# Routed tiles transposed in halves of 64 rows, in a kernel of two small transformer layers

## The chip, the cores and the metric

The kernel runs on one core of one Trainium2 chip. A core has TensorE (matmuls, "PE" in the profile, with its weight loads as "PEld"), VectorE ("DVE"), ScalarE ("ACT"), GpSimd ("POOL"), and SyncE ("SP"), whose queue issues most DMAs here. The metric is the device time of one execution in microseconds (us), lower is better. Before the change it is 555.82 us, the median of 8 runs that lie between 554.58 and 558.35.

## The reference, cut to what matters

The input is x of 8 x 256 tokens with 128 features, all in float32. Two layers follow each other; each normalises x and adds an attention part and a feed-forward part to it.

```python
xn = _layernorm(x)
x = x + scan_layer(xn) + ternary_ffn(xn)        # layer 0
xn = _layernorm(x)
x = x + ttt_attention(xn) + moe(xn)             # layer 1

# moe, the part around the change: E = 8 experts, 2 of them for each token, FF = 512
scores = sigmoid(xf @ gate_w.T + gate_b)
top_scores, top_idx = top_k(scores, 2)
hdn = gelu(xf @ w1[e] + b1[e])                  # for each expert e
y = hdn @ w2[e] + b2[e]
out = sum of the two chosen y, weighted, + 0.1 * shared expert
```

The attention of layer 1 keeps a small weight matrix W for each of 16 heads and updates it by a gradient step for each chunk of 64 tokens, so chunk n + 1 needs the W that chunk n has left.

## The kernel before, in words

**Tiles.** A tile is 128 rows of tokens on the 128 partitions. Layer 1's attention runs as 16 "units" (4 chunks x 4 pairs of batch rows), one after the other in a software pipeline: in each turn of the loop at L1303 one unit does its keys and states, the one before it its gradient and its update of W, and the one before that its outputs. The matrices between these steps go through TensorE, VectorE and GpSimd in turn.

**The routed experts.** Each token is written twice to a buffer in DRAM (xg_dram), sorted by expert. NJ = 39 tiles of 128 rows are then read back, three at a time: GJ = 3, NG = 13 groups. For a group, routed_tokens (L824) loads xg, three tiles with a token in each partition. routed_tokens_T (L832) transposes them, since the first matmul needs the features on the partitions: TensorE's transposes at L837 write one bank of PSUM, pxg, and one copy of ScalarE at L853 brings it to xgT in SBUF. For each tile j, routed_first (L855) multiplies xgT with the expert's first matrix (phd, four matmuls at L861) and applies the gelu (rhid, four ScalarE instructions at L866), and routed_second (L871) multiplies with the second one (pyr, L876). routed_sums (L882) adds the bias on VectorE (ys, L887), and a scattering DMA of GpSimd (L163) writes the rows to y_dram. routed_step (L909) strings these together: the transposes of group g + 1 are asked for in the step of tile 3g + 1, ahead of phd of tile 3g + 2 and of pyr of tile 3g + 1. The expert's weights, ew, come by DMA (L821) three tiles ahead, into four buffers.

**The order.** The order on VectorE and SP is that of the code. On TensorE and ScalarE a scheduler that knows the dependencies places the instructions, until the last unit, from where these two go by hand as well. The routed steps are the filler of the units' turns: `filler()` (L1319) puts a given number of them between the units' steps (the tables SLOTS and ROUTED).

**PSUM.** Eight banks: a pool "two" of two pairs of banks for the units, and a pool "bank" of four single banks for all else: pxg, phd, pyr, the units' po (L1258), and the shared expert's tiles. A tile of the pool takes over the bank of an earlier one, and TensorE waits until that one has been read.

**What stands elsewhere in the code.** transpose_pairs (L985) transposes the units' keys and outputs (pxkT, poT) in halves of 64 rows, the two halves into two banks; TensorE's line is L995, ScalarE's copies L999. Further lines that the prediction names: L982 (pk, pv: the units' projections, 512 columns wide), L1011 (pq), L1026 (pz, pzq: W applied, 64*64 matmuls), L1193 and L1200 (pw, pb), L1212 and L1213 (W and B on VectorE), L1094 (u), L1247 (o), L1259 and L1266 (po), L1181, L1273 (the residual). L496 is a copy of the first layer norm.

Of the kernel before, what the change touches and what calls it, by code (L numbers as in the profile page):

```python
# [17 lines left out]
P = 128  # L18
B, S, D = 8, 256, 128
# [16 lines left out]
GJ = 3  # L36
# [42 lines left out]
def tile_two_layers(ctx: ExitStack, tc: tile.TileContext, t: dict, out: bass.AP):  # L79
    nc = tc.nc  # L80
# [10 lines left out]
    def bank(name):  # L91
        return ps1.tile([P, 512], F32, tag="bank", name=name)
# [4 lines left out]
    def resident(name, shape):  # L97
        return const.tile(shape, F32, tag=name, name=name)
# [14 lines left out]
    ident = resident("ident", [P, P])  # L113
# [308 lines left out]
    with (  # L422
# [149 lines left out]
        for two in range(NBP // 2):  # L572

            pxp = bank("pxp").rearrange("p (b s) -> p b s", b=2)
            for half in range(2):
                for i in range(2):
                    b = 2 * (2 * two + i)
# [69 lines left out]
        for par in range(2):  # L647
            q = slice(par * 64, par * 64 + 64)
# [166 lines left out]
    ew, xg, xgT, hidden, ysum, unsummed, ats = {}, {}, {}, {}, {}, [], {}  # L815
# [15 lines left out]

    def routed_tokens_T(g):  # L832
        if g < NG:
            pt = bank("pxg")[:, : GJ * P].rearrange("p (j q) -> p j q", j=GJ)
            src = xg.pop(g)
            for j in range(GJ):
                nc.tensor.transpose(pt[:, j, :], src[:, j, 0:D], ident)  # L837
            ats[g] = side["moe"].tile([P, GJ], I32, tag="ats", name="ats", bufs=3)

            def places():  # L840

                first = small.tile([P, GJ], F32, tag="first", name="first")
                nc.vector.tensor_tensor(
                    first, src[:, :, D + 1], tile_rank[:, g * GJ : (g + 1) * GJ], ALU.is_equal
                )
                nc.vector.scalar_tensor_tensor(
                    ats[g], first, -float(B * S), src[:, :, D], ALU.mult, ALU.add
                )
                known.append(g)

            quiet.append(places)
            xgT[g] = side["moe"].tile([P, GJ, P], F32, tag="xgT", name="xgT")
            nc.scalar.copy(xgT[g], pt)  # L853

    def routed_first(j):  # L855
        w = ew[j]
# [52 lines left out]
    def routed_step(j):  # L909
        if j == 0:  # L910
            routed_tokens_T(0)
            routed_first(0)
        if j % GJ == 0:
            routed_tokens(j // GJ + 2)
        routed_sums()
        expert_weights(j + 3)
        if j % GJ == 1:
            routed_tokens_T(j // GJ + 1)
        if j + 1 < NJ:
            routed_first(j + 1)  # L920
        if j < NJ:
            routed_second(j)
# [380 lines left out]
    for u in range(units - 1):  # L1303
# [3 lines left out]
        z, g, o = live.get(u), live.get(u - 1), live.pop(u - 2, None)  # L1307
# [82 lines left out]
    o, g, z = live[units - 3], live[units - 2], live[units - 1]  # L1390
# [202 lines left out]
```

## Time and profile before

| what | us |
|---|---|
| median of 8 runs | 555.82 (554.58 to 558.35) |
| the profiled execution | 557.71 |
| its span, first to last instruction | 556.0 |
| TensorE busy | 524.4 (94%) |
| VectorE busy | 405.6 (73%) |
| GpSimd busy | 293.4 (53%) |
| ScalarE busy | 259.1 (47%) |
| TensorE busy from 290 to 480 us, where the transposes lie | 184.3 of 190 |
| the 39 transposes, first and last start | 296.4 and 472.9 |

A line of instructions in the profile names the line of the code, the engine, the operation, the tile that is written <- those read, the shape, and the count. A busy TensorE is a row of pipelined matmuls: one takes 0.27 us from start to end, but the next starts after 0.11 us, so start times are compared here and not durations. A matmul of float32 shows as two records, a transpose as one. In the timeline a row begins with its start in us and the time from its first start to its last end; a bracket at its end gives the idle time before it and what ended it.

### The profile page before, as it was taken

The page shows a single profiled execution, that of the slowest core. Times are in us where ns is not written, and L with a number is a line of the kernel's source. Part 1 is how long each engine was busy: PE and PEld are TensorE (multiplying, and loading weights), DVE is VectorE, ACT ScalarE, POOL GpSimd, SP SyncE. Part 2 cuts the span into 40 slices and gives each one's busy share as a digit, 9 for nine tenths or more (in the row PEclk, how much of TensorE's full clock was granted, in tenths as well). Part 3 has the DMA queues.
Part 4 walks back from the last instruction along what each step waited for, and adds up shares of the span by engine and source line. Part 5 has one row for each costly group of instructions (what it writes and reads, how often), then busy time and mean ns, then how long its engine had stood idle before and what let it go on. Part 6 is the DMA issues. An engine that isn't in the chain of part 4 may idle for free. (4 is left out here: it accounts for less than half of the span.)

```text
span 556.0 us, 14196 instructions
## 1 busy us (share of the span) xinstructions
PE 524.4 (94%) x5891; PEld 363.9 (65%) x5891; DVE 405.6 (73%) x649; ACT 259.1 (47%) x472; POOL 293.4 (53%) x258
## 2 busy tenths in 40 slices
PE   6999999999999999999988999999999999998785
PEld 3443655465455645667767888887887777878674
DVE  5599353556951377585889798979889877769995
ACT  4655544324430452232625364462645454462695
POOL 6208102862491125725486576575865747384852
PEclk9999999999999999999999999999999999999899
DMA  7910200000000000000053554452543534300402
GB/s 271 399 62 27 63 1 2 30 10 2 11 16 16 1 0 25 17 0 2 16 176 103 146 153 135 150 182 94 171 153 106 155 115 139 101 17 5 133 22 77
DMA packets 25201, 45.89 MB, mean 83 GB/s; under 512 B 3876, under 2 KB 16298, under 8 KB 24625
## 3 DMA queue, kind: packets, MB, share of 16 engines
q1 hardware_dynamic: 22864, 40.75, 22.7%
q0 software_dynamic: 2272, 4.24, 2.3%
q8 instruction: 46, 0.75, 0.6%
q14 instruction: 19, 0.15, 0.1%
HBM read 38.30 MB, written 7.13 MB: 82 GB/s over the span
## 5 line engine op out<-in xcount | busy, mean ns | idle before, releaser
L293 PE MATMUL pm<-g,h 128*128 128x512 f32 x256 | 113.6, 595 | 0.0
L175 POOL TENSOR_TENSOR rstd<-rs_v,neg_half 128x16 f32<-128x16 f32 x31 | 93.1, 3003 | 2.6
L293 PEld LDWEIGHTS pm<-g,h 128*128 128x128 f32 x256 | 48.2, 190 | 59.7 <-issue 57.0
L1118 POOL TENSOR_TENSOR gx<-xh,gam 128x1024 f32<-128x1024 f32 (+1 forms) x17 | 37.9, 2228 | 68.7 <-DVE er L1117 51.1
L866 ACT ACTIVATE rhid<-phd,ew 128x128 f32<-128x128 f32 x156 | 44.6, 373 | 40.1 <-PE phd L861 27.3
L297 ACT ACTIVATE g<-pm,cols 128x512 f32<-128x512 f32 x32 | 22.0, 687 | 75.9 <-PE pm L293 75.9
L174 POOL TENSOR_SCALAR rs_v<-var 128x16 f32<-128x16 f32 x31 | 7.3, 235 | 82.8 <-DVE var L1054 82.1
L1054 DVE TENSOR_REDUCE var<-sq 128x16 f32<-128x1024 f32 (+1 forms) x33 | 38.9, 1181 | 9.4 <-ACT sq L1048 9.4
L163 POOL DMA_INDIRECT y_dram<-ys,ats x39 | 40.7, 1044 | 8.9 <-issue 8.8
L861 PE MATMUL phd<-xgT,ew 128*128 128x128 f32 x312 | 43.1, 280 | 1.2 <-DMA ew<-in_moe_w 1.1
L861 PEld LDWEIGHTS phd<-xgT,ew 128*128 128x128 f32 x312 | 39.1, 192 | 7.4 <-issue 4.9
L1048 ACT ACTIVATE sq<-o 128x1024 f32<-128x1024 f32 (+1 forms) x17 | 17.1, 1011 | 53.6 <-DVE o L1037 53.6
L876 PE MATMUL pyr<-ew,rhid 128*128 128x128 f32 x312 | 41.4, 276 | 0.0
L163 POOL DMA_INDIRECT xg_dram<-xn,slot x32 | 35.9, 1121 | 8.6 <-issue 7.4
L1119 POOL TENSOR_TENSOR gx<-gx,u 128x1024 f32<-128x1024 f32 (+1 forms) x17 | 38.4, 2257 | 1.3
L876 PEld LDWEIGHTS pyr<-ew,rhid 128*128 128x128 f32 x312 | 38.0, 192 | 0.6 <-issue 0.5
L1094 DVE TENSOR_TENSOR u<-rows_b,pv 128x1024 f32<-128x1024 f32 x16 | 19.5, 1219 | 19.6 <-PE pv L982 19.6
L1266 PE MATMUL po<-wo,oT 128*128 128x128 f32 x256 | 31.4, 276 | 0.7 <-ACT oT L999 0.7
L982 PE MATMUL pk<-wk,xnT 128*128 128x512 f32 x64 | 31.4, 610 | 0.7 <-DVE xh L1037 0.5
L982 PE MATMUL pv<-wv,xnT 128*128 128x512 f32 x64 | 31.4, 614 | 0.0
L1011 PE MATMUL pq<-xnT,wq 128*128 128x256 f32 x128 | 30.8, 383 | 0.6 <-DVE B L1213 0.6
L1266 PEld LDWEIGHTS po<-wo,oT 128*128 128x128 f32 x256 | 29.9, 192 | 1.1 <-ACT oT L999 1.1
(233 smaller groups left out, 1058.7 us busy)
## 6 DMA issues: line engine op xcount, KB each, us to landing
ew<-in_moe_w SPq DMA_DIRECT2D x39, 578.0 KB, 3.9
xg<-xg_dram SPq DMA_DIRECT2D x39, 65.0 KB, 2.5
h<-in_h SPq DMA_DIRECT2D x2, 1024.0 KB, 8.5
yc<-y_dram SPq DMA_DIRECT2D x6, 256.0 KB, 4.1
rows_g<-in_rows_g SPq DMA_DIRECT2D x1, 1024.0 KB, 7.7
rows_b<-in_rows_b SPq DMA_DIRECT2D x1, 1024.0 KB, 7.8
w<-in_w SPq DMA_DIRECT2D x3, 256.0 KB, 3.0
x<-in_x SPq DMA_DIRECT2D x3, 256.0 KB, 5.6
```

What stands on the lines that cost most here:

```text
L163: ins = nc.gpsimd.indirect_dma_start(**what).ins
L175: turn[:] = [nc.gpsimd.tensor_tensor(dst, v[:, :width], neg_half[:, :width], ALU.pow).ins]
L293: nc.tensor.matmul(pm, lhsT=w[:, k, m * P : (m + 1) * P], rhs=s[src][:, k, :], start=(k == 0), stop=(k == 3),)
L861: nc.tensor.matmul(ph[:, ms], lhsT=w[:, ms], rhs=xgT[j // GJ][:, j % GJ, :], start=True, stop=True)
L866: nc.scalar.activation(hid[:, m, :], ph[:, ms], AF.Gelu, bias=w[:, C_EB1 + m : C_EB1 + m + 1])
L876: nc.tensor.matmul(py, lhsT=hid[:, m, :], rhs=w[:, C_EW2 + m * D : C_EW2 + (m + 1) * D], start=(m == 0), stop=(m == 3),)
L982: nc.tensor.matmul(pp[:, j, :], lhsT=xT, rhs=w[:, j * 512 : (j + 1) * 512], start=True, stop=True)
L1011: nc.tensor.matmul(pq[:, i, :], lhsT=wq[:, (h0 + i) * P : (h0 + i + 1) * P], rhs=xnT[n][:, 2 * half : 2 * half + 2, :], start=True, stop=True,
L1054: nc.vector.tensor_reduce(v[:, heads], sq[:, heads], AX.X, ALU.add)
L1118: nc.gpsimd.tensor_tensor(g, xh, gam2[:, k], ALU.mult)
L1119: turn[:] = [nc.gpsimd.tensor_tensor(g, g, self.t[:, k], ALU.add).ins]
L1266: nc.tensor.matmul(self.po, lhsT=self.oT[:, hp, :], rhs=wo[:, hp, :], start=False, stop=(hp == HH - 1),)
```

## The change

Each tile is transposed in two halves, rows 0 to 63 and 64 to 127. The first halves of a group's three tiles go to one bank, the second halves to another one, so a group takes two banks of the pool of four in place of one. Six transposes of 64 rows take the place of three of 128, and two copies of ScalarE (128 partitions x 3 x 64 elements each) that of one of 128 x 384; each writes its half of xgT's columns.

```diff
     def routed_tokens_T(g):
         if g < NG:
-            pt = bank("pxg")[:, : GJ * P].rearrange("p (j q) -> p j q", j=GJ)
             src = xg.pop(g)
+
+            pts = []
+            for b in range(2):
+                pts.append(bank("pxg")[:, : GJ * 64].rearrange("p (j q) -> p j q", j=GJ))
             for j in range(GJ):
-                nc.tensor.transpose(pt[:, j, :], src[:, j, 0:D], ident)
+                for b in range(2):
+                    rb = slice(b * 64, b * 64 + 64)
+                    nc.tensor.transpose(pts[b][:, j, :], src[rb, j, 0:D], ident[rb, rb])
...
             xgT[g] = side["moe"].tile([P, GJ, P], F32, tag="xgT", name="xgT")
-            nc.scalar.copy(xgT[g], pt)
+            for b in range(2):
+                nc.scalar.copy(xgT[g][:, :, b * 64 : b * 64 + 64], pts[b])
```

In the built program VectorE, SP and GpSimd keep their order. On TensorE the scheduler makes these moves besides: in group 1 one matmul of pq goes ahead of phd; in group 4 the first half-transpose of pxkT goes ahead of pyr; in group 11 the six halves stand with the three first ones in front, and of the phd matmuls that stand between other work there one is placed later, as is one of the next tile.

## The prediction

> **What bounds the kernel now.** I read the page's busy shares first, then the table of windows for the stretch in which the change lives, then the tile view of pxg, and last the timeline around single groups. "Group g" (0 to 12) is one call of routed_tokens_T: three routed tiles.
>
> The chain of waits on the page is no help: it holds 1 us. The busy shares and the windows (sum of each engine in us per stretch) are:
>
> ```profile
> PE 524.4 (94%) x5891; PEld 363.9 (65%) x5891; DVE 405.6 (73%) x649; ACT 259.1 (47%) x472; POOL 293.4 (53%) x258
> ...
> 290.00:360.00 70.00, 67.39 (x981) 54.70 (x982) 62.71 (x83) 35.26 (x79) 43.70 (x28) 1.00 0.47 143
> 360.00:420.00 60.00, 59.04 (x910) 47.50 (x902) 50.54 (x70) 28.70 (x64) 42.50 (x29) 1.00 0.46 145
> 420.00:480.00 60.00, 57.88 (x881) 47.22 (x879) 47.63 (x64) 30.82 (x69) 37.28 (x26) 1.00 0.41 130
> ```
>
> From 290 to 480 us TensorE is busy 184.3 of 190 us at full clock, VectorE 160.9, ScalarE 94.8. All 13 groups lie there. So what lengthens TensorE's queue lengthens the kernel, unless a wait of TensorE on something else follows soon and swallows it. What the diff touches is small:
>
> ```profile
> L837 PE MATMUL pxg<-ident,xg x39: 272/273/331, 296.4 to 472.9; 128*128 128x128 f32 x39
> L853 ACT COPY xgT<-pxg x13: 463/478/498, 299.0 to 473.8; 128x384 f32<-128x384 f32 x13
> ```
>
> 273 ns is a latency; transposes start 0.11 us apart (303.31 to 303.63 for three). The whole step holds TensorE for 13 x 0.33 = 4.3 us.
>
> **The transposes themselves.** The kernel already has the new form, 64 rows into two banks, in L995 (poT, pxkT). TensorE's timeline around group 4:
>
> ```profile
> 346.62 0.49 PE L837 MATMUL pxg<-ident,xg 128*128 128x128 f32 x3
> 346.95 1.06 PE L861 MATMUL phd<-xgT,ew 128*128 128x128 f32 x8
> 347.84 1.06 PE L876 MATMUL pyr<-ew,rhid 128*128 128x128 f32 x8
> 348.83 0.71 PE L995 MATMUL pxkT<-ident,xk 64*128 64x64 f32 x16
> 349.48 0.70 PE L982 MATMUL pv<-wv,xnT 128*128 128x512 f32 x1
> ```
>
> Differences of the start times give all prices. phd to pyr, eight records of full matmuls, is 0.89; pyr to pxkT, also eight, is 0.99: entering the 64-row form costs 0.10. Sixteen halves take 0.65 until the next engine operation starts (348.83 to 349.48). They go in pairs: at 307.24 the first pair starts, at 307.35 the second, and further ones 0.06 apart. Three pairs are then 0.65 - 5 x 0.062 = 0.33 or 0.34, as much as the three full transposes. After a 64-row block the first full matmul is long: phd at 307.89, behind poT, needs 0.99 for its eight records (pyr starts at 308.88), against 0.89. Leaving therefore costs another 0.10. So a group between full matmuls pays 0.33 before and 0.10 + 0.33 + 0.10 = 0.53 after: +0.20 us. It has two neighbours of another kind:
> - behind poT (groups 3 and 8) the kernel is in the form already: before, 330.93 to 331.95 for 16 halves and three transposes, 1.02; after, 0.65 + 3 x 0.062 = 0.83, and phd later by 0.10: -0.09.
> - behind the 64*64 matmuls of L1026 (groups 2, 7, 10) the three transposes take 0.39 (440.53 to 440.92), already with a slow first. After: 0.33 + 0.10, with the same way in: +0.05. That a change from 64*64 to 64*128 costs what one to 128*128 costs is assumed; L1181 to L995 at 540.74 has the same 0.15 us start to start.
>
> The trace speaks here against a rule. The Trainium skill, TensorEngine Tiling (Array Packing), section Overview, gives operands of at most 64 up to twice the speed; alone it would make the sum 13 x 0.165 = 2.1 us less, an estimate from that page. The same page, Tiling Modes, says that a change of the tiling mode drains TensorE, which is what the 0.10 at the entry looks like, and its first gotcha that row tiling raises the pressure on PSUM.
>
> **The banks.** "bank" is a pool of four. A group now takes two, so each later tile in the ring waits for another predecessor. I compared the waits of the two built programs, and put each new one against the start and end times of before. The second half's bank waits for ys (L887) or a gelu (L866) that ended 1.8 to 4.3 us earlier in groups 2 to 9; phd's and pyr's waits on ys, a gelu or the residual (L1273) ended 0.6 to 2.8 us earlier. These cost nothing: the cover is that slack. pyr's new wait for the group's first copy is different, since ScalarE is in order. Group 3:
>
> ```profile
> 331.94 1.02 ACT L999 COPY oT<-poT 128x1024 f32<-128x1024 f32 x1
> 332.84 0.50 ACT L853 COPY xgT<-pxg 128x384 f32<-128x384 f32 x1
> ...
> 332.85 1.06 PE L876 MATMUL pyr<-ew,rhid 128*128 128x128 f32 x8
> ```
>
> The copy stands behind two long ones (xqT, oT) and starts at 332.84; pyr is ready at 332.85. A copy of 128x192 has no row. Copies of 256 (L496, 372 ns) and 384 (482 ns) give 0.86 ns an element, so 0.32 us; not below 0.28 (the cheapest small ScalarE row, 283 ns for 128x96), not above 0.37 (256). Its end, 333.16, and 0.05 for the semaphore (gelu ends at 452.33, phd starts at 452.38) put pyr at 333.21: +0.36. A matmul that waited is followed late (452.38: four records up to poT take 0.65, 0.10 more than full ones with the entry), +0.10. Group 8 is the same (copy 405.44, pyr 405.45). So +0.46 each, -0.09 included; bounds +0.3 (no late second, shortest copy) and +0.55. Behind pyr queue the mix of L1259/L1266 and pw, for which VectorE waits (W at 337.07), so nothing hides it.
>
> Group 4: its copy starts at 347.73 and would be done at 348.05; pyr comes at 347.84 + 0.20. But the scheduler also puts the first half of pxkT ahead of pyr: one more way in and out, 0.10 + 0.15 + 0.10 = +0.35, below which the wait disappears. Bounds 0.1 (it merely replaces the wait) and 0.4. In group 1 one pq matmul moves ahead of phd and covers the gelu it now waits for (303.89). In group 11 the second halves wait for the gelu that ended at 452.33, and phd for the first copy: about +0.35 at 452.4.
>
> **The copies.** ScalarE's copies start 0.37 us before the next operation (332.84 to 333.21). Two of 192 take about 0.05 more than that: 13 x 0.05 = 0.7 us on an engine half idle. The later gelus serve a pyr that runs a step later. Without that cover (group 3's gelus on the path) it would be 0.1 a group. SP's, POOL's and VectorE's orders are unchanged; no DMA is added or moved.
>
> **What swallows some of it.** TensorE's waits behind groups:
>
> ```profile
> 379.56 0.72 PE L995 MATMUL poT<-ident,o 64*128 64x64 f32 x16 [0.56 <-DVE o L1247]
> ...
> 426.50 0.72 PE L995 MATMUL poT<-ident,o 64*128 64x64 f32 x16 [0.42 <-ACT rhid L866]
> ...
> 458.41 0.91 PE L861 MATMUL phd<-xgT,ew 128*128 128x128 f32 x6 [1.12 <-DMA ew<-in_moe_w]
> ```
>
> Before 379.56 VectorE ran without a gap from 369.1; so group 6 (372.4) is hidden. The same for group 9 (423.8), where o ended at 426.35. The weights of 458.41 were issued at 452.93, behind a ys that stands behind u, which waited for pv (450.25), not for group 11: its 0.35 is hidden. Group 0 is followed by a wait of 1.3 for xh. If those covers go, +0.2, +0.2, +0.35 and +0.2 come back. All other delays lie ahead of a VectorE wait on TensorE (u on pv at 351.50, 400.12, 450.25, 477.53), so both shift and nothing catches up.
>
> **The sum.** Groups 1, 4, 5, 12: 4 x 0.20 = 0.80; 2, 7, 10: 0.15; 3 and 8: 0.92; group 4's extra excursion 0.35; copies 0; groups 0, 6, 9, 11: 0. Together +2.2 us. The profiled execution took 557.71 (span 556.0 and 1.7 around it) and would take 559.9. It stands 1.9 above the median of the runs, 555.82; the same +2.2 on the median is 558.0, +0.4%. 0.3%, about what a measurement of this kernel can tell from no change, is 1.7 us.
>
> **The rivals.**
> - It comes to nothing. The late second matmul may belong to longer blocks, a short block may enter cheaper, and more of TensorE's 5.5 us of waits in this stretch may swallow. With the entry alone (4 x 0.10), the waits 2 x 0.3 and 0.1 for group 4: +1.1, less 0.4 swallowed: 556.5. For it: each term is a tenth. Against: entry and exit show at every L995 block of this stretch.
> - Faster. If three pairs are left and entered without a stop, they cost 0.19 in place of 0.33: 13 x 0.14 = -1.8, and 554.0 if pyr also finds its copy done. It decides where a way in and out together is below 0.14; the rows say 0.20, and 3 and 8 would still wait.
> - The ring of four is too short. If VectorE falls over 2 us behind in its ys additions, the second half's bank waits stop TensorE in seven or eight groups, at about 0.5 us each: +4 more, 562. It needs ys later by the slack of 1.8 to 4.3 us; delays of TensorE move VectorE along, which speaks against.
>
> **How the numbers follow.** My forecast has 0.60 (own range 557.2 to 559.5), nothing 0.20, faster 0.10, the ring 0.10. The range of 554.8 to 560.8 leaves out most of the ring case and part of the faster one. Slower by over 0.3% (above 557.5): most of the forecast and the ring, 0.66; within: the second case and the low end of the forecast, 0.23; faster 0.11.
>
> **What would show it.** L853 has 26 copies near 0.32; pxg has 78 halves, three pairs 0.06 to 0.11 apart; phd behind them takes 0.99; pyr of groups 3 and 8 idles about 0.4 with ScalarE's xgT as releaser; the waits at 379.56, 426.50 and 458.41 shrink. TensorE's stretch from 290 to 480 is 2 us longer, the tail behind it the same. I am wrong if TensorE waits for ys at the halves, or if that stretch keeps its length.

## The result, and the profile after

| | kernel before | changed kernel |
|---|---|---|
| median of the runs, us | 555.69 (46 runs, 554.05 to 558.35) | 558.16 (16 runs, 557.08 to 560.65) |
| profiled execution, us | 557.71 | 558.34 |
| its span, us | 556.0 | 556.6 |

The ratio is 1.0042, with a 95% interval of 1.0032 to 1.0052: slower by 2.5 us of median. The prediction said 558.0. Note at once what does not fit: the two profiled executions lie only 0.6 us apart, where the prediction added 2.2 to the one and expected 559.9 of the other. That gap is taken up below.

First the busy shares of the page and the table of windows of the changed kernel (length, then busy us and instructions of PE, PEld, DVE, ACT, POOL, then the granted TensorE clock, the DMA share, GB/s):

```profile
PE 526.0 (95%) x5930; PEld 362.7 (65%) x5930; DVE 405.2 (73%) x649; ACT 260.2 (47%) x485; POOL 293.8 (53%) x258
...
290.00:360.00 70.00, 67.08 (x961) 53.44 (x960) 61.49 (x81) 35.65 (x84) 43.76 (x28) 1.00 0.47 142
360.00:420.00 60.00, 58.92 (x937) 47.30 (x937) 49.90 (x71) 27.98 (x66) 40.78 (x28) 1.00 0.46 146
420.00:480.00 60.00, 59.19 (x890) 47.10 (x889) 48.60 (x63) 31.44 (x71) 39.07 (x27) 1.00 0.41 129
```

TensorE works 39 instructions more, ScalarE 13 more; VectorE, POOL and the moved bytes stay. From 290 to 480 us TensorE is busy 185.2 us instead of 184.3, in a stretch of the same length that holds slightly less of the program. The clock is full here in both.

The tile view of pxg shows the new form (minimum, median and maximum in ns, first and last start), and who waited for it:

```profile
L842 PE MATMUL pxg<-ident,xg x78: 221/223/273, 296.5 to 473.9; 64*128 64x64 f32 x78
L859 ACT COPY xgT<-pxg x26: 303/325/352, 299.0 to 475.0; 128x192 f32<-128x192 f32 x26
...
who waited for it (us, times):
...
  PE pyr L882: 0.6, 2
```

78 halves, 26 copies of 325 ns (0.32 was predicted), and a wait of pyr that the kernel before has nowhere: twice, 0.6 us in all. Its first place is group 3, on the timeline:

```profile
331.96 1.16 PE L867 MATMUL phd<-xgT,ew 128*128 128x128 f32 x8
332.14 1.02 ACT L1005 COPY oT<-poT 128x1024 f32<-128x1024 f32 x1
...
333.04 0.56 ACT L859 COPY xgT<-pxg 128x192 f32<-128x192 f32 x2
...
333.43 1.16 PE L882 MATMUL pyr<-ew,rhid 128*128 128x128 f32 x8 [0.32 <-ACT xgT L859]
```

The two copies stand behind the long oT. pyr now waits for the bank that the first copy reads, and starts at 333.43 where it started at 332.85: +0.58. Group 4 shows the other change of order, one half of pxkT alone between phd and pyr:

```profile
347.73 1.16 PE L867 MATMUL phd<-xgT,ew 128*128 128x128 f32 x8
348.82 0.27 PE L1001 MATMUL pxkT<-ident,xk 64*128 64x64 f32 x1
349.02 1.16 PE L882 MATMUL pyr<-ew,rhid 128*128 128x128 f32 x8
350.11 0.71 PE L1001 MATMUL pxkT<-ident,xk 64*128 64x64 f32 x15
```

From phd to pyr it was 0.89 (346.95 to 347.84); it is 1.29.

**Step by step.** Every start of TensorE in the changed kernel was set against the start of the same instruction before. The difference grows in steps:

| group | predicted | measured on the start times of TensorE |
|---|---|---|
| 0 | 0, a wait for xh behind it | 0.00 |
| 1 | +0.20 | +0.19 (pq behind phd: 305.86 to 306.04) |
| 2, 7, 10 | 3 x 0.05 | 0.00, -0.07, 0.00 |
| 3 | +0.46 | +0.50 (0.19 to 0.69) |
| 4 | +0.20 and +0.35 | +0.19 (phd) and +0.40 (pyr, the rest of pxkT) |
| 5 | +0.20 | +0.20 (1.27 to 1.47) |
| 6 | 0, swallowed at poT | 1.47, 1.67 at phd, 1.47 again at poT |
| 8 | +0.46 | +0.54 (1.40 to 1.94) |
| 9 | 0, swallowed at poT | 1.94, 2.14 at phd, 1.85 at poT |
| 11 | 0, swallowed by the weights | 1.94, up to 2.44 at phd, then 1.05 behind the weights |
| 12 | +0.20 | +0.20 (0.98 to 1.18) |

Up to group 10 the prediction has 0.20 + 0.15 + 0.92 + 0.55 + 0.20 = 2.02 and the trace 1.94. The two swallowed excursions of groups 6 and 9 are the plainest. The timeline of the changed kernel has

```profile
374.33 1.16 PE L867 MATMUL phd<-xgT,ew 128*128 128x128 f32 x8
...
381.02 0.71 PE L1001 MATMUL poT<-ident,o 64*128 64x64 f32 x16 [0.36 <-DVE o L1253]
```

where the wait for VectorE's o was 0.56: it lost the 0.20 that group 6 added.

**What the table does not explain** is group 11. In the profile before, TensorE waited 1.12 us at 458.41 for expert weights. In the changed kernel's that wait is missing altogether, and 1.07 us come back at once; the shift falls from 2.1 to 1.05. So the prediction's "swallowed" is too weak a word, and the sum of 2.2 cannot be read off these two profiles. Half a microsecond more comes back in the last 36 us, where the granted clock is 0.87 in the profile before and 0.95 in the changed kernel's. The experiments therefore had two questions: are the steps' prices right, and what is the wait for weights?

### The profile page after: what moved, and what is told of

Its sections match the earlier page's. It is cut to its first block, busy times and chain, and to the rows that moved or that the text cites. A ratio compares the mean times of both kernels' runs of the same rounds, so it can differ in the third digit from the quotient of the medians.

```text
span 556.6 us, 14286 instructions
## 1 busy us (share of the span) xinstructions
PE 526.0 (95%) x5930; PEld 362.7 (65%) x5930; DVE 405.2 (73%) x649; ACT 260.2 (47%) x485; POOL 293.8 (53%) x258
```

## The experiments

All times are medians; each ratio is to the kernel before on the same chip, with its 95% interval, and a difference written with a plus sign is worked out from the ratio unless the text says otherwise. An experiment's "shift" is the difference of matched start times, as in the table above.

**The kernel before, again.**

> The kernel of before, unchanged, to learn what of its first profile is of that one execution. Ratio 1.000 within 0.1%. The first profile was 2.0 us above the median. If its wait of 1.12 us for the weights at 458.4 and the granted clock of 0.87 in its last 36 us belong to that execution alone, the wait is absent or much shorter here, and the span is nearer to 554. If the wait is the kernel's own, it stands here too, and then the changed kernel has won about 1 us there.

Median 555.70 (12 runs), ratio 0.9991 (0.9974 to 1.0009); the profiled execution took 557.50, and in its trace TensorE waits 1.22 us for the weights at 458.40. The 12 times are nine from 554.56 to 555.99 and three from 557.50 to 557.70. Two separate groups are not shown by that: of the 46 runs in the table of the result 15 lie between 556.2 and 557.3. Both profiled executions of this program are of its upper end.

**Two banks and two copies, but full transposes.**

```diff
-            pt = bank("pxg")[:, : GJ * P].rearrange("p (j q) -> p j q", j=GJ)
+            for b in range(2):
+                pts.append(bank("pxg")[:, : 2 * P].rearrange("p (j q) -> p j q", j=2))
...
-                nc.tensor.transpose(pt[:, j, :], src[:, j, 0:D], ident)
+                nc.tensor.transpose(pts[j // 2][:, j % 2, :], src[:, j, 0:D], ident)
...
+            nc.scalar.copy(xgT[g][:, 0:2, :], pts[0])
+            nc.scalar.copy(xgT[g][:, 2:GJ, :], pts[1][:, 0:1, :])
```

> Two banks and two copies without the 64-row form: tiles 0 and 1 of a group go to one bank, tile 2 to the other, by full transposes. If the cost of the change is entering and leaving the 64-row form (0.20 us at groups 1, 4, 5, 12, 0.35 for the lone half of pxkT) plus the wait of pyr for the first copy in groups 3 and 8, then only the wait is left, somewhat longer since the first copy is of 256 elements (0.37 us): 2 x 0.5 = 1.0 us, and up to 0.4 at group 4, where pxkT still goes ahead of pyr in part: +1.0 to +1.4 us on 555.7. If the form alone costs, it is as before (within 0.3 us). If the ring of banks alone costs, it is as the changed kernel (+2.4).

557.66 (12 runs), 1.0028 (1.0012 to 1.0044): +1.6 us without a half transpose of a routed tile, a little over the +1.0 to +1.4 expected. The scheduler's moves are nearly those of the change (pq in group 1; in group 4 two halves of pxkT ahead of pyr, where the change has one; in group 11 a similar order), and the wait for the first copy is there too (table of TensorE's waits: who waits, for whom, us, times, longest; then the timeline of group 4):

```profile
PE pyr L880 <- ACT xgT L856: 0.5, 2, 0.3
```

```profile
348.03 0.28 PE L999 MATMUL pxkT<-ident,xk 64*128 64x64 f32 x2
348.25 1.16 PE L880 MATMUL pyr<-ew,rhid 128*128 128x128 f32 x8
```

Its shift grows by 0.54 in group 3, 0.35 in group 4, 0.54 in group 8 and 0.29 in group 11. The steps of groups 3 and 8 are the wait for the first copy. That of group 4 is again a way into and out of the 64-row form, by halves of pxkT that the scheduler moved. So all of these steps follow from the second bank, and they are more than half of the change's cost, but they are not all waits.

**Two copies, all else as before.**

```diff
-            nc.scalar.copy(xgT[g], pt)
+            for b in range(2):
+                nc.scalar.copy(xgT[g][:, :, b * 64 : b * 64 + 64], pt[:, :, b * 64 : b * 64 + 64])
```

> One bank and full transposes as before, but two copies of 192 elements each instead of one of 384. The orders of all engines are those of before. My theory says the extra ScalarE time (about 0.05 us a group) is hidden: within 0.3 us of before. A rival in which ScalarE's extra instructions count would give 13 x 0.05 to 13 x 0.2, that is +0.7 to +2.6 us.

556.04 (12 runs), 0.9993 (0.9977 to 1.0009): the copies cost nothing, as predicted. This run also gave, by chance, what was missing: the order on TensorE is that of the kernel before, the profiled execution took 556.03, a typical time, and its trace has no wait for weights. phd starts behind po, not at 458.41:

```profile
456.98 0.83 PE L862 MATMUL phd<-xgT,ew 128*128 128x128 f32 x6
```

Set against this execution, the changed kernel's trace ends 2.30 us later, and the times of the two profiled executions are 2.31 apart.

**The lone half put back.** A dependency without a semaphore keeps the first half of group 4's pxkT behind the last pyr of tile 10; nothing else of the change is touched.

```diff
-                nc.tensor.transpose(
+                ins = nc.tensor.transpose(
...
+                if name == "xkT" and hp == b == 0 and max(seconds, default=0) == 10:
+                    tc.add_manual_dep(ins, seconds[10].name, ... NoSync ...)
```

> The changed kernel, but in group 4 the 16 half-transposes of pxkT stay together behind pyr, by an order that TensorE keeps without a wait. By my sum this takes away one way into and out of the 64-row form, 0.35 us, less the wait for the first copy that shows up instead (at most 0.1): 0.25 to 0.4 us below the changed kernel, so +2.0 to +2.2 us on before. In the profile pyr of that group starts right behind phd or at the end of the first copy. If the excursion costs nothing, it is as the changed kernel, +2.4.

558.42 (12 runs), 1.0036 (1.0021 to 1.0052), which the timing cannot tell from the change itself. On the timeline of this kernel group 4 is

```profile
347.64 1.16 PE L867 MATMUL phd<-xgT,ew 128*128 128x128 f32 x8
348.70 1.16 PE L882 MATMUL pyr<-ew,rhid 128*128 128x128 f32 x8
349.79 0.71 PE L1001 MATMUL pxkT<-ident,xk 64*128 64x64 f32 x16
350.44 1.12 PE L988 MATMUL pv<-wv,xnT 128*128 128x512 f32 x2
```

From phd to pv it takes 2.80 us, against 3.02 in the changed kernel (347.73 to 350.75) and 2.53 before. The excursion of one half thus costs 0.22 net, since without it a short wait of pyr for the copy shows (1.06 from phd to pyr, not the 0.99 of a block after the 64-row form).

**What entering and leaving costs.** Two kernels with the same work: the changed kernel with two spare full transposes a group, into columns of the banks that nothing reads, once behind the six halves and once between their pairs. The order on all engines is otherwise the same.

```diff
                 nc.tensor.transpose(pts[b][:, j, :], src[rb, j, 0:D], ident[rb, rb])
-            for j in range(2):
-                nc.tensor.transpose(spare[j], src[:, j, 0:D], ident)
+                if j < 2:
+                    nc.tensor.transpose(spare[j], src[:, j, 0:D], ident)
```

> The changed kernel with two full transposes more per group, written to unused columns of the two banks, behind the six halves. It serves as the base of the next one: 13 x 2 x 0.11 = 2.9 us of TensorE more, part of it hidden; the scheduler also moves some groups, the same in both. So about +4 to +5.5 us on before.

> The same instructions as in the kernel with the two full transposes behind the halves, and otherwise the same order on every engine, but the full ones stand between the pairs of halves, so the 64-row form is entered and left three times in a group and not once. By the start times of before a group takes 0.37 us more: 13 x 0.37 = 4.8 us if all counts, 3.3 if the four groups before a wait hide it. So +3.3 to +4.8 us on the kernel with them behind. If entering and leaving were free, no difference.

Behind: 560.03 (6 runs), 1.0070 (1.0056 to 1.0083), just under what was expected of it. Between: 564.37 (5 runs), 1.0158 (1.0142 to 1.0173). The difference is 4.3 us, in the medians and in the spans (558.2 and 562.5), inside the expected 3.3 to 4.8. 26 further ways in and out make it, 0.17 us each, on average over the groups, the ones that a wait covers included. On the start times of TensorE the shift between the two grows by 4.9 us from 300 to 476 us, 0.19 each. In the tile views the same instructions grow longer, first those of "behind", then of "between":

```profile
L844 PE MATMUL pxg<-ident,xg x78: 221/223/273, 296.3 to 475.0; 64*128 64x64 f32 x78
...
L846 PE MATMUL pxg<-ident,xg x26: 272/328/330, 296.6 to 475.4; 128*128 128x128 f32 x26
```

```profile
L844 PE MATMUL pxg<-ident,xg x78: 221/272/276, 295.9 to 479.7; 64*128 64x64 f32 x78
...
L846 PE MATMUL pxg<-ident,xg x26: 327/329/332, 296.1 to 479.5; 128*128 128x128 f32 x26
```

The median half goes from 223 to 272 ns, and every full transpose that follows a half takes 0.33 instead of 0.27. That is the price that the prediction took from the neighbours of poT and pxkT (0.20 for both ways), measured by itself. The Trainium skill, TensorEngine Tiling (Array Packing), section Tiling Modes, says in words that a change of mode drains TensorE; these two kernels give it a number for this form. The factor of up to two in its Overview does not show in a block this short: in the changed kernel three pairs hold TensorE for 0.33 us (347.40 to 347.73), as the three full transposes did.

**Parts of the groups.** The new form in groups 3 and 8 alone, and in groups 1, 4, 5 and 12 alone; the other groups run as before.

```diff
+            new = g in (1, 4, 5, 12)
+            if new:
...
+            else:
+                pt = bank("pxg")[:, : GJ * P].rearrange("p (j q) -> p j q", j=GJ)
```

> Halves, two banks and two copies in groups 3 and 8 alone, all others as before; the orders of all engines are those of before. These are the groups where the 64-row form costs nothing, since poT is in it already (-0.09 each), and where pyr waits for the first copy. By the wait: +0.46 to +0.6 each, +0.9 to +1.2 us on before. If the form were the whole cost: -0.2 us.

> Halves, two banks and two copies in groups 1, 4, 5 and 12 alone. There the halves stand between full matmuls, no copy is waited for, and group 4 has the lone half of pxkT: 4 x 0.20 + 0.35 = +1.15 us on before by the form's entry and exit. If waits for copies or banks were the whole cost: 0.

Both miss. Groups 3 and 8: 557.95 (12 runs), 1.0030 (1.0012 to 1.0047), +1.7 where 0.9 to 1.2 was expected, though the interval of 0.7 to 2.6 us holds that too. Groups 1, 4, 5, 12: 558.24 (6 runs), 1.0040 (1.0027 to 1.0054), +2.2 where 1.15 was, outside the interval. Their sum is well above the whole change. The traces say why the steps themselves are nevertheless right. In the first kernel the shift grows by 0.58 from phd to pyr in both groups, as in the changed one; but its profile starts the stretch about 1 us late, from a place that no edit touches (windows of this kernel, then of the kernel before; the column after POOL is the granted clock):

```profile
258.00:262.00 4.00, 3.59 (x36) 2.80 (x36) 1.83 (x6) 2.45 (x4) 1.26 (x1) 0.87 0.01 4
262.00:266.00 4.00, 4.00 (x53) 2.73 (x52) 2.86 (x14) 3.21 (x6) 0.00 (x0) 0.70 0.00 0
```

```profile
258.00:262.00 4.00, 3.59 (x73) 2.79 (x64) 1.83 (x7) 1.93 (x3) 1.26 (x1) 1.00 0.02 4
262.00:266.00 4.00, 4.00 (x55) 2.49 (x54) 3.39 (x14) 3.97 (x7) 0.00 (x0) 1.00 0.00 0
```

Over these 8 us TensorE ran at 0.70 to 0.87 of its clock in that one execution, and the shift goes from -0.54 to +1.15. The execution took 559.61, as far above the median of its kernel. In the second kernel group 4 adds 0.57 and group 5 0.20, as in the changed one. And in both TensorE waits for the weights of group 11, 1.41 and 0.95 us. Against the copies execution, which does not wait there, the shift rises over that place by 1.6 us in the first kernel (2.22 to 3.82) and by 1.1 in the second (0.84 to 1.98). So in these two executions the excess over the steps is the wait. The change, two banks and the lone half put back do not wait there.

**The wait for the weights.** The load in question is one transfer of 578 KB. From issue to landing it took (the DMA view of 452 to 456.6 us; size, then us) before, in the copies kernel and in the changed kernel:

```profile
ew<-in_moe_w SPq DMA_DIRECT2D x1, 578.0 KB, 5.3
```

```profile
ew<-in_moe_w SPq DMA_DIRECT2D x1, 578.0 KB, 4.0
```

```profile
ew<-in_moe_w SPq DMA_DIRECT2D x1, 578.0 KB, 3.8
```

Between its packets lies one of another queue. In the profile before, a packet of 16,384 bytes on the instruction queue starts at 456.22, 3.29 us after the issue, when the load has only its last packets left, and takes 0.96 us. In the DMA view of 456.2 to 456.26, and in that of 456.6 to 457.5, it is seen first to begin and then, with everything else silent, to leave a single small packet behind it:

```profile
q8 instruction: 1, 0.02, 99.9%
```

```profile
DMA packets 1, 0.00 MB, mean 0 GB/s; under 512 B 1, under 2 KB 1, under 8 KB 1
```

That lone packet of 4 bytes, at 457.16, is the last of the 16 that the load ends with. In the copies kernel the instruction packet starts at 456.25, just behind the load's last small packet, and the stretch after it is empty:

```profile
DMA packets 0, 0.00 MB, mean 0 GB/s; under 512 B 0, under 2 KB 0, under 8 KB 0
```

So whether TensorE waits for about 1 us goes with where this one packet falls among those of the load. That the last packet of the load stands behind it on the same one of the 16 DMA engines is read from this order in time; the views do not name the engine. In all traces with the wait (before, again, groups 3 and 8, groups 1, 4, 5 and 12) the instruction packet starts 2.75 to 3.6 us after the issue, with packets of the load still to come; in the changed kernel and in the one with the lone half put back it starts 0.5 us after it, and the load lands in 3.8 and 4.2 us. (With two banks and full transposes it starts at 3.4, behind the last small packet as in the copies kernel, and the load took 4.0.) Counting TensorE's records, matmuls and weight loads, tells why: the packet falls on the 8,909th to 8,927th in all these kernels, wherever that is in the work, and the changed kernel has about 70 more by then, six a group. The program has 46 such packets, on average 258 records apart. The count is not exact: the packet near 368 us falls on record 6,429 in one profile of the kernel before and on 6,455 in the other, and the one near 392 us on 7,177 before and on 7,087 in the changed kernel. The Trainium skill, Runtime: NRT & Kernel Launch, section Instruction fetch mechanics, has the program streamed in blocks of 16 KiB, 256 instructions, and the cost of a block's boundary mostly hidden; here two packets lie 256 records apart where nothing else disturbs (record 4,104 at 290.7 us, 4,360 at 294.2). Whether the cost of this one packet is hidden depends on where it falls: in the same order of work TensorE waited in two executions of the kernel before and not in that of the copies kernel.

**The same with the fetch moved.** If this is right, TensorE instructions at the start of the program, where TensorE is idle until 5.3 us, must move the packet of 456 us.

```diff
+    spare = bank("spare")
+    for i in range(32):
+        nc.tensor.transpose(spare[:, 0:64], ident[0:64, :], ident[0:64, 0:64])
     neg_half = resident("neg_half", [P, H])
```

> The kernel before with 32 spare half transposes of the identity at its very start, where TensorE waits for the first input until 5.3 us; nothing else moves on any engine, and the output is untouched. Why: in every trace TensorE's 8,903rd to 8,927th record falls together with a packet of 16,384 bytes on the instruction queue, 0.93 to 0.96 us long; in the kernel before it starts 3.3 us after the issue of the weights of 458 us, at the end of their packets, and the load then took 5.2 to 5.6 us to land; in the changed kernel, with about 70 more records ahead of it, it starts 0.5 us after the issue, and the load took 3.8. The 64 records here should move the packet about as far. Theory (the wait for weights is this packet in the load's way): the load lands in 3.6 to 4.2 us, TensorE does not wait for it, and the runs show none of the group at 557.5 that about a quarter of the kernel before's show: median 0 to -0.5 us. Rival (the late landing has another cause): it lands in over 5 us and the 1.1 to 1.2 us wait is there.

In its trace the load is issued at 465.60 and the packet starts at 466.38, 0.78 us after it instead of 3.29: it moved as forecast. The timeline (first phd behind the weights, and its weight load) and the view of 466.3 to 466.42:

```profile
470.11 0.91 PE L864 MATMUL phd<-xgT,ew 128*128 128x128 f32 x6
```

```profile
470.07 0.74 PEld L864 LDWEIGHTS phd<-xgT,ew 128*128 128x128 f32 x6 [0.31 <-issue]
```

```profile
q8 instruction: 1, 0.02, 64.2%
```

Most of the wait for weights is gone, but not all. The load raises its semaphore at 469.97, 4.37 us after the issue and a little over the 3.6 to 4.2 expected. TensorE's load of phd's weights, which that semaphore releases, idles 0.31 us ahead of it (the view writes "issue" there) and phd itself 0.15; in the kernel before it was 1.28 and 1.12. The time shows nothing: 573.57 (12 runs), 1.0001 (0.9973 to 1.0030). This run and the next three were on two chips on which the kernel before takes 573 to 574 us, with the granted clock below full in several stretches (0.96 from 260 to 300 us), and the interval is as wide as the effect that was looked for. On these chips the time follows the granted clock of the run: of the 17 runs of the kernel before 571.16 us goes with 0.990 and 577.03 with 0.980. A straight line of the time in that clock, fitted with one slope for both kernels, leaves +0.2 us between them (-0.2 to +0.7), an estimate from these 29 runs. That the packet moved is shown; that moving it takes most of the wait away rests on one execution of this kernel and on those listed above; that it makes the kernel faster is not shown.

**Loads a step earlier.** A fifth buffer for the weights, in both kernels (and two for xg, for room):

```diff
-            w = side["moe"].tile([P, NEW], F32, tag="ew", name=f"ew_{j}", bufs=4)
+            w = side["moe"].tile([P, NEW], F32, tag="ew", name=f"ew_{j}", bufs=5)
...
-            xg[g] = side["moe"].tile([P, GJ, ROW], F32, tag="xg", name="xg", bufs=3)
+            xg[g] = side["moe"].tile([P, GJ, ROW], F32, tag="xg", name="xg", bufs=2)
```

> The kernel before with five buffers for the expert weights in place of four (two for xg in place of three, so that they fit). A load then waits for the results of the tile before last and is issued a step, some 4 us, earlier. The profiled executions of the kernel before have TensorE waiting 1.1 to 1.2 us for weights at 458.4, of the copies kernel not at all, in the same program order: the load took 5.3 and 4.0 us to land. Theory (an accident of that one load, of some executions only): the wait is gone in every execution, and the median 0.2 to 1.0 us below the kernel before. If the wait belongs to few executions: no difference. Rival (earlier loads collide with the token loads and the scatters): slower by 0.5 or more.

> The changed kernel with the same five buffers. The question is how much of the measured +2.5 us is the sum of my steps and how much the wait for weights that the shifted work meets. If the sum is right: five_after is 2.2 to 2.6 us above five_before (group 11's 0.35 has lost its cover). If the weights' wait carried the difference: about 1 us or less above it.

With the fifth buffer the kernel before takes 580.24 (6 runs), 1.0100 (1.0066 to 1.0134) of it: worse, where 0.2 to 1.0 us less was expected. The late wait is gone, but the scheduler, told that weights come earlier, puts the first expert tiles earlier too, and TensorE now waits there, for the list that routes the tokens and for the first weights:

```profile
PE pw L1193 <- DVE first L843: 2.6, 2, 2.5
PE phd L861 <- DMA ew<-in_moe_w: 2.6, 1, 2.6
```

The changed kernel with the fifth buffer takes 582.20 (6 runs), 1.0146 (1.0110 to 1.0182), 2.0 us above the former by the medians, near the 2.2 to 2.6 expected. In the traces TensorE's shift between these two rises from 0.51 at 325 us to 2.95 at pw of 480 us: +2.44 with no wait for weights near group 11 in either, the steps of groups 3 and 8 being 0.58 each. At equal clock, by such a straight line, the 12 runs lie 2.8 us apart (2.1 to 3.5). With clock dips in both and so few runs this is agreement and not proof.

**The groups that should cost nothing.**

> The new form in groups 0, 6, 9 and 11 alone, the ones that the prediction costed at nothing. Theory (waits of TensorE for VectorE, ScalarE and the weights cover them): 0 to +0.4 us, the trace back at the kernel before's times at poT of 379.56 and 426.50; in group 11, where the second half of the tile's phd goes behind pw, it may end on either side of the weights' wait, -1.0 to +0.4. Rival (the covers are not there in most executions): 0.2 + 0.2 + 0.2 + 0.35 = +0.95.

574.74 (12 runs), 1.0010 (0.9986 to 1.0034): +0.6 by the ratio, and the interval holds both forecasts. At equal clock (17 runs of the kernel before, from 570.98 at 0.992 to 577.03 at 0.979) the straight line leaves 0.0 us between the two, -0.4 to +0.4: that is the theory's 0 to +0.4 and not the rival's +0.95. The trace says where. Against the trace of the kernel with the moved fetch (the kernel before but for the 32 spare transposes, taken on a chip with similar dips) the shift is 1.47 ahead of group 6, 1.65 at its phd and 1.45 at the pxkT behind; 1.53 ahead of group 9, 1.73 at its phd, 1.45 at poT. Both covers hold. In group 11 the shift rises to 1.97 and stands at 1.26 at pw, 1.48 behind it; but the trace that it is set against waits 0.31 us there for weights, and this one does not, so group 11 would add about 0.3 to an execution without that wait.

## Why the prediction was right

**The prices of the form** (0.20 for a way in and out, no gain from pairs) were read off neighbours that already had it. Groups 1, 5 and 12 and the first part of group 4 measured 0.19, 0.20, 0.20 and 0.19, and the pair of kernels with spare transposes gave 0.17 a round trip over all groups.

**The new wait** of pyr for the first copy stood in the prediction as the chain copy start, 0.32 of copy, semaphore, and 0.10 for the late second matmul: +0.46. It measured +0.50 and +0.54. It belongs to the banks and not to the halves: with full transposes into two banks the same two steps are +0.54 each.

**The lone half** of pxkT was put at +0.35 and measured +0.40; taken out it gives back only 0.22, because the wait that it replaced then shows. The prediction had said that the wait disappears below it.

**Behind L1026** (groups 2, 7, 10) 3 x 0.05 was wrong in size: the trace gives 0.00, -0.07 and 0.00.

**The covers** of groups 6 and 9 held to the hundredth. That of group 11 did not, and here a step failed: "its 0.35 is hidden" by the wait for weights, "issued at 452.93", which the prediction took for a fixed part of the program. It hangs on where a packet of the instruction queue falls. In the changed kernel it is absent, and the median of the kernel before is near the time of the execution without it (556.03 of the copies kernel) and not near those with it (557.50, 557.71). Against the execution without the wait, group 11's 0.35 is not covered (the shift is 2.14 ahead of it, at 450 us, and 2.48 behind it, where the copies kernel's phd stands at 463.97 and the changed one's at 466.45); with group 12 it is 2.63, and 0.3 comes back in the tail.

**The sum** was made against 557.71 and carried over to the median as it stood. The number came out right within 0.2 us in part by luck: against the copies execution two errors are small and opposed, about +0.35 in group 11 and -0.3 in the tail. The tail is of these executions and not of the change: its granted clock is 0.90 in the copies kernel's profile (from 520 us on) and 0.95 in the changed kernel's. What the tail does to the medians is not shown. The profiled execution itself was forecast at 559.9 and took 558.34: there the missing wait (1.1 us) and the tail's clock (0.87 before, 0.95 after) make up the difference. The prediction's sign that TensorE's stretch from 290 to 480 us becomes 2 us longer is likewise met only against the execution without the wait (2.6 us); against the profile that it was read from it is 1.2.

**The rivals.** "Comes to nothing" needed short blocks that enter cheaper and a copy that pyr does not wait for; "faster" needed pairs without a stop. The start times show neither. "The ring of four is too short" needed halves that wait for ys; no pxg transpose waits for VectorE in the trace.

**What stays open** is how often the kernel before runs into its wait: only profiled executions tell, and the times do not fall into two groups that could be counted. The two kernels with part of the groups come out about 1 us above the sum of their steps. The wait in their profiles is long enough for that, but whether their other runs have it is not on record, and the timed intervals (0.7 to 2.6 and 1.5 to 3.0 us) are wide. None of the versions beats the kernel before.

## What to carry to other kernels

On an engine that is 94% busy a form that is the same length per piece still costs its borders: count how often a short block of it stands between others, and price each border from start-to-start times of neighbours that already have the form. Splitting a tile over two banks changes whom later tiles wait for, and the wait to look for is the one behind an in-order engine's long copies; here the two waits cost 1.04 us, and the ways in and out of the form that nothing covered 0.78, or 1.18 with the lone half. Before a wait in a profiled execution is used as a cover, look whether the median of the runs stands where that execution does: if it does not, the wait may belong to that execution and not to the program.

## What the runs showed of the hardware that was not expected

- A block of TensorE's program (16,384 bytes, 0.93 to 0.96 us on one DMA queue) can hold up the last packets of a weight load, which then lands in 5.2 to 5.6 us and not in 3.8 to 4.4. It comes at nearly the same count of TensorE's records in the traces listed with the wait for the weights and in that with the moved fetch (the 8,909th to 8,931st), so a change in that count ahead of it moves it against the work: about 70 records moved it by 2.8 us, 64 at the start of the program by 2.5.
- A block of a single 64-row transpose holds TensorE for 0.20 us to the next matmul's start (348.82 to 349.02), of six for 0.33 (347.40 to 347.73): most of a short block is its borders.
- The granted clock fell to 0.70 for some microseconds in the middle of one execution, in a stretch that runs at 1.00 before and in the changed kernel, and cost 1.7 us (the shift goes from -0.54 to +1.15). Where a shift is read off two traces, start behind such a place.
